# A fused attention and expert kernel: the last pair of heads in two halves of its queries, and other places for three other pieces of work

## The chip, the cores and the metric

The kernel runs on one core of one Trainium2 chip. A core has five engines, each with its own queue of instructions: TensorE (PE in the profile, with its weight loads PEld), VectorE (DVE), ScalarE (ACT), GpSimd (POOL) and SyncE (SP, which here only issues DMAs). An engine takes its instructions in the order in which they are written; a semaphore holds one back until what it needs is done. The metric is the device time of one execution in microseconds (us); lower is better.

## The reference, cut to what matters

```python
# x (4, 1024, 256); 16 heads of 16; 8 experts, top 2, capacity 640
q, k, v = (heads of x @ w.T for w in (wq, wk, wv))
q_mag, k_mag = softplus(q), softplus(k)
q_embed = q_mag * (cos, sin)(pos * inv_freq)               # 32 numbers per head
k_embed = k_mag * (cos, sin)(pos * inv_freq + clip(bias))
attn = softmax(q_embed @ k_embed.T / 4)                    # per batch and head, 1024 x 1024
x = layernorm(x + (attn @ v) @ wo.T)
gates = softmax(x @ router_w + router_b)                   # 4096 tokens, 8 experts
# each token goes to its two best experts; an expert takes its first 640 tokens in order
out = gelu(buf @ w1 + b1) @ w2 + b2                        # per expert, on its 640 slots
x = layernorm(x + sum over the token's experts of gate * out)
```

## The kernel before

**Attention in pairs and steps.** Two heads make a pair. A batch has 8 pairs, the four batches 32 (numbers 0 to 31). A pair is walked in 8 steps of key tiles, 256 steps in all. A *unit* is what is walked at a time: a whole pair (8 steps, all 1024 queries), or half of a pair's queries (4 steps, 512 queries each). Before, the pairs 0 to 3 are walked as two units each, all others as one. `starts` holds the first step of each unit.

In step n of unit w and key tiles c the program writes, in this order: up to two *score* products of a later unit (`score_half`, L755, each followed on DVE by a reduction to a row maximum, L759); `key_scores(w, c, 0)`, two products into a double bank of the pool `st` (L795); a third score; `key_scores(w, c, 1)`; a fourth score; in `exponentials` four short products that subtract the row maxima (L809), and two exponentials of 128x1024 on ACT (L816); `weighted_values` of the step before (av, 16 instructions, L836); further scores; pieces of a later unit's maxima (`max_parts` on DVE and ACT; `max_rows`, four transposes `mp` on PE and a copy `mt` on ACT); and what the table `todo` has for step n. The pool `st` has two buffers, so `key_scores` waits for the exponentials of the step before. Scores use three banks, which they share with the other products.

The scores are spread over the steps by a small plan: each unit's scores must be given two steps before it starts, and each step takes as many as the tightest due time asks for. A whole unit has 32, half a unit 16. Half units need their own maxima, and so their own `max_parts` and `max_rows`.

**Loads.** `load_qk(i)` issues 12 DMAs on SP (8 of 128 KB, 4 of 256 KB), the first six for the pair's first head, the others for the second. Its tile has three buffers, shared with the tables and weights of the lead-in, and with the expert weights. It is called for pair i at the first step of pair i - 2.

**Behind a half batch.** `collect` sends the weighted values and their sums away over SP. `over_sums` then loads the sums (`den`), takes reciprocals on DVE, stores them (`over`), loads them spread over the partitions (`r`, eight DMAs), and multiplies. For the second half of a batch's heads this runs in steps 1, 2, 5 and 6 of the next batch. Then `project` (PE, and an addition on DVE) and `statistics` follow, and `finish_batch`: normalization, transposes, the router, the choice of two experts, the running count of slots, and the indirect DMAs on POOL that scatter the tokens' rows into `slots_in`.

**The end of attention.** The second half of the last batch's heads goes another way: `normalize` (transposes of the av tile, reciprocals and products on DVE into `os`), `turn_back` (transposes of `os`, a copy on ACT), then `project`, `statistics`, and `finish_batch` in two halves of 512 tokens, `one` and `two`. A `run(one)` takes the generator to its next `yield`: reciprocal roots (1), their correction (2), normalizing and transposing (3 to 6), router products (7), and so on to the four scatters of two DMAs each (17 to 20). Only after the last scatter are the first expert's slots loaded (L1183) and transposed (L1194), and the products of the experts begin.

**Lead-in.** Before step 0 the program builds the first pair's queries and keys on the chip. `moving` moves rows into place on PE, with a copy on ACT; `mq1` is the generator for the second half of the queries, `q1` and others are the embeddings. `once` copies weights on DVE and so frees the buffer that pair 1 is loaded into.

Of the kernel before, what the change touches and what calls it, by code (L numbers as in the profile page):

```python
# [10 lines left out]
F32 = mybir.dt.float32  # L11
# [17 lines left out]
def kernel(  # L29
# [72 lines left out]
    with ExitStack() as actx:  # L102
# [627 lines left out]
        nms, mts, avs, pts = {}, {}, {}, {}  # L730


        units = []
        starts, lasting = [], []
        for i in range(B * NU):
            for h in range(2) if i < NU // NF else (None,):
                starts.append(starts[-1] + lasting[-1] if units else 0)
                units.append((i, *divmod(i // (NU // NF), NF), i % (NU // NF), h))
                lasting.append(NT if h is None else NT // 2)
# [158 lines left out]

        def normalize(w, rotate=False):

            _, b, f, p, _ = units[w]
            if p == 0:
                oss[b, f] = p1.tile([P, NT, P], F32, tag="os", name=f"os_{b}_{f}")
            av_sb = avs.pop(w)
            ps = bank(f"avp_{w}", rotate)
            for i in range(4):
                nc.tensor.transpose(
                    ps[:, i * P : (i + 1) * P], av_sb[:, i * P : (i + 1) * P], ident
                )
            r = small.tile([P, 4, 4], F32, tag="rden", name=f"rden_{w}")  # L910
            nc.vector.reciprocal(r, ps.rearrange("p (i s c) -> p i s c", i=4, c=32)[:, :, :, HD])
            for n in range(2):
                nc.vector.tensor_tensor(
                    oss[b, f][:, 4 * n : 4 * (n + 1), 32 * p : 32 * (p + 1)].rearrange(
                        "p i (h d) -> p i h d", d=HD
                    ),
                    ps.rearrange("p (i n h c) -> p n i h c", i=4, n=2, h=2)[:, n, :, :, 0:HD],
                    r[:, :, 2 * n : 2 * n + 2].unsqueeze(3).to_broadcast([P, 4, 2, HD]),
                    ALU.mult,
                )  # L920

# [81 lines left out]
        with tc.manual_schedule():  # L1003
            bias_angles()
            once("k", 0)
            for i in range(2):
                transpose_x(0, i, rotate=True)
            nc.scalar.dma_start(wv_sb, wv)
            for w in "kq":
                load_twice(w, 1, nc.scalar)  # L1010
            for _ in key_table(0):
                pass
            once("q", 0)

            made = {}

            def first(w, h):
                return embedding(
                    0, 0, w, h, fast=(w, h) != ("q", 1), tab=cs if w == "q" else kt0,
                    pauses=(KC - 1,), rotate=True, apart=h == 1, made=made,  # L1020
                )

            def moving(w, h):
                return move_first(w, halves[h], made[w, h])

            k0, q0, k1, q1 = first("k", 0), first("q", 0), first("k", 1), first("q", 1)
            for work in (k0, k0):
                run(work)
            for i in range(2, 4):
                transpose_x(0, i, rotate=True)  # L1030
            table = key_table(1)
            for work in (q0, table, table, q0, k0, table, k1, q0, table, k1):
                run(work)
            mk0, mq0 = moving("k", 0), moving("q", 0)
            for work in (mk0, mq0, mk0, mq0, q1):
                run(work)

            for i in range(2):
                score_half(0, 2 * i, 0, True)
            for work in (k1, q1, q1):  # L1040
                run(work)
            for i in range(2, 4):
                score_half(0, 2 * i, 0, True)
            for work in (mk0, mq0, mk0, mq0, k0, q0):
                run(work)
            mk1 = moving("k", 1)
            run(mk1)
            for i in range(4):
                score_half(0, 2 * i + 1, 0, True)
            for work in (mk1, mk1, mk1, k1):  # L1050
                run(work)
            vals = [values_in_two(0, 0, h, rotate=True) for h in range(2)]
            for h in range(2):
                for i in range(4):
                    score_half(0, 2 * i + h, 1, True)
                    if (h, i) in ((0, 3), (1, 1)):
                        run(vals[0])
            for _ in vals[1]:
                pass
            mq1 = moving("q", 1)  # L1060
            for _ in range(4):
                run(mq1)
            for _ in max_parts(0):
                pass
            max_rows(0, rotate=True)
            run(q1)
            for h in range(2):
                store_table(0, h, cs[:, :, halves[h]])
                store_table(1, h, kt0[:, :, halves[h]])
            once("k", 1)  # L1070
            once("q", 1)
            load_qk(1)
            late_constants()
# [10 lines left out]
        with tc.manual_schedule():  # L1084
            for n in range(NS):
                w, c = step_of[n]
                b, p, t = n // (NU * NT), n // NT % NU, n % NT
                if n % NT == 0 and n > 0 or n == NT // 2:
                    i = n // NT + 2
                    if i < B * NU:  # L1090
                        load_qk(i)
                    elif i - B * NU < 2:
                        experts[i - B * NU] = expert_weights(i - B * NU)


                third_last, others[0] = others[0], False
                items = [(score_half, *x) for x in ahead[n]]
                first, third, fourth, rest = items[:2], items[2:3], items[3:4], items[4:]
                if third_last:
                    third, fourth = [], third + fourth  # L1100
                for f, *args in first:
                    f(*args)
                if parts:
                    run(parts)
                    parts = None
                tiles = [key_scores(w, c, 0)]
                for f, *args in third:
                    f(*args)
                tiles.append(key_scores(w, c, 1))
                for f, *args in fourth:  # L1110
                    f(*args)
                exponentials(w, c, tiles)
                if n > 0:
                    weighted_values(*step_of[n - 1])
                for f, *args in rest:
                    f(*args)
                if n + 2 in starts:
                    parts = max_parts(starts.index(n + 2))
                    run(parts)
                if n + 1 in starts:  # L1120
                    max_rows(starts.index(n + 1))
                if c == 1 and w > 0 and not by_rows(w - 1):
                    normalize(w - 1)
                for f, args in todo.get(n, ()):
                    f(*args)
                if b > 0 and (p, t) in FINISH:
                    if b not in finishing:
                        finishing[b] = finish_batch(b - 1)
                    next(finishing[b], None)
            weighted_values(*step_of[NS - 1])  # L1130


        with tc.manual_schedule():
            b, n = B - 1, NT // 2
            normalize(len(units) - 1, rotate=True)
            for i in range(2):
                turn_back(b, 1, i, rotate=True)
            for j in range(2):
                project(b, 1, j, rotate=True)
                statistics(b, j)  # L1140
            one, two = (finish_batch(b, rotate=True, lo=lo, n=n) for lo in (0, n))
            run(one)
            project(b, 1, 2, rotate=True)
            for _ in range(3):
                run(one)
            project(b, 1, 3, rotate=True)
            for j in range(2, 4):
                statistics(b, j)
            for _ in range(3):
                run(one)  # L1150
            run(two)
            for _ in range(2):
                run(one)
            run(two)
            for _ in range(4):
                run(one)
            run(two)
            for _ in range(3):
                run(one)
            for _ in range(n):  # L1160
                run(one)
            for _ in two:
                pass
            second_factors()
            nc.scalar.preload_act_table_set("gelu_and_others")
# [297 lines left out]
```

## Time and profile before

| What | Value |
|---|---|
| median of 3 runs | 1423.62 us (1423.34 to 1423.67) |
| the profiled execution | 1425.13 us |
| its span, first to last instruction | 1423.3 us |
| PE busy | 1365.4 us (96%) |
| DVE busy | 885.8 us (62%) |
| ACT busy | 740.8 us (52%) |
| POOL busy | 408.3 us (29%) |
| score products (L755), 1024 | 383.4 us busy, mean 434 ns |
| score reductions (L759), 1024 | 646.9 us busy, mean 683 ns |
| mean granted TensorE clock | 0.983 |

All durations come from one profiled execution. Busy times of PE are modelled at their ends, so a busy PE is not PE at its peak; step lengths are therefore read as distances between the starts of the same instruction in two steps. In section 2 of the page the span is cut into 40 slices of 35.6 us, and a digit is the busy share of a slice in tenths; PEclk is the clock that TensorE was granted. A timeline line has the start, the duration, engine, line, operation, what it writes and reads, and in square brackets how long the engine was idle before it and what ended that. SPq lines are DMA issues. A table by stage has from:to, length, then for PE, PEld, DVE, ACT and POOL the busy time and number of instructions, then clock, share of the DMA engines and GB/s.

### The profile page before, as it was taken

What the parts mean: (1) busy time and instruction counts of PE and PEld (TensorE: products, weight loads), DVE (VectorE), ACT (ScalarE), POOL (GpSimd) and SP (SyncE); (2) the same over time, 40 slices, a digit from 0 to 9 for tenths busy, and PEclk for the clock granted to TensorE, in tenths of its full rate; (3) what the DMA queues carried; (4) which work ended last, traced back from release to release, by engine and by line L of the source; (5) the groups of instructions that cost most, each with busy time, mean ns of one, the idle gap of its engine ahead of it and who ended that gap; (6) DMA issues with size and microseconds to landing.
All of it is one profiled execution on the core that took longest, in us unless ns stands there. A gap on an engine that the chain in (4) does not pass through costs nothing. (4 is left out here: it accounts for less than half of the span.)

```text
span 1423.3 us, 24542 instructions
## 1 busy us (share of the span) xinstructions
PE 1365.4 (96%) x9362; PEld 863.9 (61%) x9362; DVE 885.8 (62%) x1931; ACT 740.8 (52%) x1025; POOL 408.3 (29%) x427
## 2 busy tenths in 40 slices
PE   7999999999999999999999999999996399999998
PEld 4655555655655565565556556655643277777776
DVE  7667666667876666777856577887734433333335
ACT  5665676565566656556575665656463122222221
POOL 5261043340002646100065530000310314444443
PEclk9999999999999999999999999999998599999999
DMA  6776476374543746454466462225210436334211
GB/s 192 214 206 194 141 200 189 86 228 113 138 123 96 229 143 182 112 165 97 139 184 193 106 186 70 64 74 128 75 66 1 141 114 207 111 117 135 84 44 56
DMA packets 107765, 190.20 MB, mean 134 GB/s; under 512 B 19553, under 2 KB 56642, under 8 KB 107520
## 3 DMA queue, kind: packets, MB, share of 16 engines
q1 hardware_dynamic: 97792, 169.90, 41.2%
q0 software_dynamic: 8736, 16.87, 3.9%
q10 hardware_dynamic: 1120, 1.87, 0.4%
q8 instruction: 74, 1.21, 0.4%
q14 instruction: 43, 0.35, 0.1%
HBM read 118.27 MB, written 73.63 MB: 135 GB/s over the span
## 5 line engine op out<-in xcount | busy, mean ns | idle before, releaser
L759 DVE TENSOR_REDUCE nm<-s 128x1 f32<-128x512 f32 x1024 | 646.9, 683 | 234.1 <-PE s L755 226.0
L816 ACT ACTIVATE pt<-st 128x1024 f32<-128x1024 f32 x512 | 496.1, 1021 | 364.1 <-PE st L809 363.6
L755 PE MATMUL s<-qk 128*128 128x512 f32 x1024 | 383.4, 434 | 3.6 <-DVE nm L759 2.2
L795 PE MATMUL st<-qk 128*128 128x512 f32 x1024 | 303.8, 398 | 2.6 <-ACT pt L816 2.6
L836 PE MATMUL av<-pt,va 128*32 128x256 f32 x4096 | 274.7, 385 | 0.5 <-ACT pt L816 0.5
L755 PEld LDWEIGHTS s<-qk 128*128 128x128 f32 x1024 | 177.9, 188 | 110.5 <-DVE nm L759 49.4
L795 PEld LDWEIGHTS st<-qk 128*128 128x128 f32 x1024 | 182.7, 188 | 63.5 <-ACT pt L816 29.2
L836 PEld LDWEIGHTS av<-pt,va 128*32 128x32 f32 x4096 | 107.1, 109 | 107.0 <-issue 61.6
L692 POOL DMA_INDIRECT slots_in<-held,scatter_idx x64 | 63.0, 984 | 290.9 <-DVE scatter_idx L688 213.6
L414 POOL TENSOR_TENSOR soft_q<-y_q,soft_q 128x512 f32<-128x512 f32 x15 | 19.3, 1285 | 439.7 <-ACT soft_q L410 439.7
L1364 PE MATMUL op<-w,h 128*128 128x256 f32 x640 | 144.1, 379 | 0.0
L1345 PE MATMUL hp<-slots_t,w 128*128 128x320 f32 x512 | 141.0, 437 | 0.0
L1364 PEld LDWEIGHTS op<-w,h 128*128 128x128 f32 x640 | 119.5, 190 | 15.9
L809 PE MATMUL st<-mt,ones_r 2*128 2x512 f32 x1024 | 128.8, 492 | 0.0
L1345 PEld LDWEIGHTS hp<-slots_t,w 128*128 128x128 f32 x512 | 98.4, 192 | 40.4 <-issue 1.0
L809 PEld LDWEIGHTS st<-mt,ones_r 2*128 2x128 f32 x1024 | 49.0, 182 | 88.5 <-issue 88.1
L1352 ACT ACTIVATE h<-hp,b_sb 128x640 f32<-128x640 f32 x64 | 50.8, 793 | 87.7 <-PE hp L1345 87.7
L1379 DVE TENSOR_TENSOR o<-op,b_sb 128x256 f32<-128x256 f32 x35 | 14.9, 424 | 94.7 <-PE op L1364 94.6
L1380 ACT ACTIVATE o<-o,w 128x256 f32<-128x256 f32 x35 | 17.8, 508 | 103.2 <-issue 72.3
L1382 POOL DMA_INDIRECT y_rank<-o,rows x35 | 35.9, 1024 | 101.2 <-ACT slots_t L1195 46.1
L1303 POOL DMA_INDIRECT out_dram<-row,rows x40 | 40.9, 1022 | 42.7 <-DMA out_dram<-row,rows 13.1
L420 POOL TENSOR_TENSOR e_k<-soft_k,tab_k 128x512 f32<-128x512 f32 x28 | 35.4, 1286 | 47.5 <-DMA tab_k<-table 47.1
(217 smaller groups left out, 1034.5 us busy)
## 6 DMA issues: line engine op xcount, KB each, us to landing
qk<-embed_q SPq DMA_DIRECT2D x248, 128.0 KB
qk<-embed_k SPq DMA_DIRECT2D x124, 256.0 KB
embed_k<-parts_k SPq DMA_DIRECT2D x64, 256.0 KB
embed_q<-parts_q SPq DMA_DIRECT2D x64, 256.0 KB
w<-in_w_dram SPq DMA_DIRECT2D x16, 1024.0 KB
y_rank<-zero SPq DMA_DIRECT2D x8, 1024.0 KB
tab_q<-table SPq DMA_DIRECT2D x14, 512.0 KB
tab_k<-table SPq DMA_DIRECT2D x14, 512.0 KB
```

Of the source, the lines that this page charges most:

```text
L692: nc.gpsimd.indirect_dma_start(out=scatter_views[2 * t + k], out_offset=bass.IndirectOffsetOnAxis(ap=scatter_idx[:, k, t : t + 1], axis=0) ...
L755: nc.tensor.matmul(ps, qk[:, 2 * h, lo : lo + P], qk[:, 2 * h + 1, j * HS : (j + 1) * HS], start=True, stop=True,)
L759: nc.vector.tensor_reduce(nms[w][:, i, s, j : j + 1], ps, AX.X, ALU.max, negate=True)
L795: nc.tensor.matmul(ps[:, x, :], qk[:, 2 * h + 1, k * P : (k + 1) * P], qk[:, 2 * h, q * HS : (q + 1) * HS], start=True, stop=False,)
L809: nc.tensor.matmul(tiles[t][:, x, :], ones_r[rows, :], mts[w][rows, :], start=False, stop=True,)
L816: nc.scalar.activation(pt, tiles[t], AF.Exp)
L836: nc.tensor.matmul(av[32 * s : 32 * (s + 1), to], va[f][:, k, 2 * p + h, :], e, start=(c == 0 and n == 0), stop=(last and n == 1),)
L1303: nc.gpsimd.indirect_dma_start(out=out_views[t], out_offset=bass.IndirectOffsetOnAxis(ap=to[:, 0, t : t + 1], axis=0), in_=row[:, t, :], i ...
L1345: nc.tensor.matmul(ps[:, i, 0:half], w1_sb[:, k, c * P : (c + 1) * P], s_t[:, k, i * half : (i + 1) * half], start=(k == 0), stop=(k == KC ...
L1352: nc.scalar.activation(h_t[:, c, :].rearrange("p (i n) -> p i n", i=2), ps[:, :, 0:half], AF.Gelu, bias=b1_sb[:, e, c : c + 1],)
L1364: nc.tensor.matmul(ps, h_t[:, c, t * P : (t + 1) * P], w2_sb[:, c, :], start=(c == 0), stop=(c == HC - 1),)
L1382: nc.gpsimd.indirect_dma_start(out=y_views[e * ST + t], out_offset=bass.IndirectOffsetOnAxis(ap=to[:, 1, t : t + 1], axis=0), in_=o_sb, in ...
```

## The change

Pair 31 is walked as two half units, and pairs 1 to 3 as whole units; pair 0 stays in halves. `normalize` can take half a unit. In step 253 the first half of pair 31 is normalized, at the start of step 254 its tokens are turned back, at that step's end tiles 0 to 3 are projected and their statistics taken, and in step 255 `one` makes its first stage. The order of what follows attention is rewritten accordingly. In the lead-in, `max_parts(0)` comes before the second half of the values, and three of the four stages of `mq1` come after `max_rows(0)`. The qk load at the first step of a batch (other than batch 0) moves to the batch's fourth step.

```diff
--- before.py
+++ after.py
@@ -730,10 +730,12 @@
         nms, mts, avs, pts = {}, {}, {}, {}
 
 
+
+        BY_HALF = (0, B * NU - 1)
         units = []
         starts, lasting = [], []
         for i in range(B * NU):
-            for h in range(2) if i < NU // NF else (None,):
+            for h in range(2) if i in BY_HALF else (None,):
                 starts.append(starts[-1] + lasting[-1] if units else 0)
                 units.append((i, *divmod(i // (NU // NF), NF), i % (NU // NF), h))
                 lasting.append(NT if h is None else NT // 2)
@@ -898,24 +900,27 @@
 
         def normalize(w, rotate=False):
 
-            _, b, f, p, _ = units[w]
+            _, b, f, p, half = units[w]
             if p == 0:
                 oss[b, f] = p1.tile([P, NT, P], F32, tag="os", name=f"os_{b}_{f}")
             av_sb = avs.pop(w)
             ps = bank(f"avp_{w}", rotate)
-            for i in range(4):
+
+            m, tiles = (4, (0, 4)) if half is None else (2, (4 * half, 4 * half + 2))
+            for i in range(m):
                 nc.tensor.transpose(
                     ps[:, i * P : (i + 1) * P], av_sb[:, i * P : (i + 1) * P], ident
                 )
-            r = small.tile([P, 4, 4], F32, tag="rden", name=f"rden_{w}")
-            nc.vector.reciprocal(r, ps.rearrange("p (i s c) -> p i s c", i=4, c=32)[:, :, :, HD])
-            for n in range(2):
+            ps = ps[:, 0 : m * P]
+            r = small.tile([P, 4, 4], F32, tag="rden", name=f"rden_{w}")[:, 0:m, :]
+            nc.vector.reciprocal(r, ps.rearrange("p (i s c) -> p i s c", i=m, c=32)[:, :, :, HD])
+            for n, t in enumerate(tiles):
                 nc.vector.tensor_tensor(
-                    oss[b, f][:, 4 * n : 4 * (n + 1), 32 * p : 32 * (p + 1)].rearrange(
+                    oss[b, f][:, t : t + m, 32 * p : 32 * (p + 1)].rearrange(
                         "p i (h d) -> p i h d", d=HD
                     ),
-                    ps.rearrange("p (i n h c) -> p n i h c", i=4, n=2, h=2)[:, n, :, :, 0:HD],
-                    r[:, :, 2 * n : 2 * n + 2].unsqueeze(3).to_broadcast([P, 4, 2, HD]),
+                    ps.rearrange("p (i n h c) -> p n i h c", i=m, n=2, h=2)[:, n, :, :, 0:HD],
+                    r[:, :, 2 * n : 2 * n + 2].unsqueeze(3).to_broadcast([P, m, 2, HD]),
                     ALU.mult,
                 )
 
@@ -1055,15 +1060,15 @@
                     score_half(0, 2 * i + h, 1, True)
                     if (h, i) in ((0, 3), (1, 1)):
                         run(vals[0])
+            for _ in max_parts(0):
+                pass
             for _ in vals[1]:
                 pass
             mq1 = moving("q", 1)
-            for _ in range(4):
-                run(mq1)
-            for _ in max_parts(0):
-                pass
+            run(mq1)
             max_rows(0, rotate=True)
-            run(q1)
+            for work in (mq1, mq1, mq1, q1):
+                run(work)
             for h in range(2):
                 store_table(0, h, cs[:, :, halves[h]])
                 store_table(1, h, kt0[:, :, halves[h]])
@@ -1085,12 +1090,15 @@
             for n in range(NS):
                 w, c = step_of[n]
                 b, p, t = n // (NU * NT), n // NT % NU, n % NT
-                if n % NT == 0 and n > 0 or n == NT // 2:
+
+                if t == 0 and p > 0 or t == 3 and p == 0 and b > 0 or n == NT // 2:
                     i = n // NT + 2
                     if i < B * NU:
                         load_qk(i)
                     elif i - B * NU < 2:
                         experts[i - B * NU] = expert_weights(i - B * NU)
+                if n == NS - 2:
+                    turn_back(B - 1, 1, 0)
 
 
                 third_last, others[0] = others[0], False
@@ -1127,27 +1135,31 @@
                     if b not in finishing:
                         finishing[b] = finish_batch(b - 1)
                     next(finishing[b], None)
+                if n == NS - 2:
+                    for j in range(2):
+                        project(b, 1, j)
+                        statistics(b, j)
+                    one, two = (
+                        finish_batch(b, rotate=True, lo=lo, n=NT // 2) for lo in (0, NT // 2)
+                    )
+                elif n == NS - 1:
+                    run(one)
             weighted_values(*step_of[NS - 1])
 
 
         with tc.manual_schedule():
             b, n = B - 1, NT // 2
+            run(one)
             normalize(len(units) - 1, rotate=True)
-            for i in range(2):
-                turn_back(b, 1, i, rotate=True)
-            for j in range(2):
+            for _ in range(2):
+                run(one)
+            turn_back(b, 1, 1, rotate=True)
+            for _ in range(2):
+                run(one)
+            for j in range(2, 4):
                 project(b, 1, j, rotate=True)
                 statistics(b, j)
-            one, two = (finish_batch(b, rotate=True, lo=lo, n=n) for lo in (0, n))
             run(one)
-            project(b, 1, 2, rotate=True)
-            for _ in range(3):
-                run(one)
-            project(b, 1, 3, rotate=True)
-            for j in range(2, 4):
-                statistics(b, j)
-            for _ in range(3):
-                run(one)
             run(two)
             for _ in range(2):
                 run(one)
```

## The prediction

> **What bounds the kernel now.** I read the page first, then TensorE's timeline by steps, the timeline of the passage between attention and experts, and SyncE's timeline where a batch begins.
>
> ```profile
> span 1423.3 us, 24542 instructions
> ...
> PE   7999999999999999999999999999996399999998
> ...
> PEclk9999999999999999999999999999998599999999
> ```
>
> PE is busy in every slice but those around 1067 to 1139 us, and there the granted clock drops too. Elsewhere a change pays only if it takes work or a wait from PE. Steps, from the timeline:
>
> ```profile
> 1034.94 1.07 PE L836 MATMUL av<-pt,va 128*32 128x256 f32 x16
> ...
> 1038.44 1.07 PE L836 MATMUL av<-pt,va 128*32 128x256 f32 x16
> ...
> 1063.92 0.73 PE L795 MATMUL st<-qk 128*128 128x512 f32 x2 [0.19 <-ACT pt L816]
> ...
> 1065.02 1.07 PE L836 MATMUL av<-pt,va 128*32 128x256 f32 x16
> 1068.28 1.07 PE L836 MATMUL av<-pt,va 128*32 128x256 f32 x16
> ```
>
> Four score products: 3.50 us from one av group to the next, no gap on PE. No scores (the last nine steps): still 3.26, because the second st pair waits for the second exponential. Five scores take 3.85 (69.08 to 72.92 in the same view). So a score costs 0.35 where PE is full and nothing below a floor of about 3.2.
>
> The passage, all engines:
>
> ```profile
> 1071.72 1.94 ACT L816 ACTIVATE pt<-st 128x1024 f32<-128x1024 f32 x2 [1.33 <-PE st L809]
> ...
> 1092.36 0.19 DVE L604 TENSOR_TENSOR logits<-lq,rb_sb 128x32 f32<-128x32 f32 x1 [0.18 <-PE lq L590]
> ...
> 1100.52 0.97 POOL L692 DMA_INDIRECT slots_in<-held,scatter_idx  x1 [62.46 <-DVE held L678]
> ...
> 1112.32 0.97 POOL L692 DMA_INDIRECT slots_in<-held,scatter_idx  x1 [1.89 <-DVE second L706]
> ...
> 1123.93 0.94 SPq L1183 DMA_DIRECT2D slots<-slots_in  x2
> ...
> 1128.18 3.00 PE L1194 MATMUL st<-ident,slots 128*128 128x128 f32 x10 [17.92 <-DMA slots<-slots_in]
> ```
>
> One serial chain: step 254's exponentials, routing of the first half, eight scatters, routing of the second half (late by 1.89), eight scatters, reload. The start of batch 1, SyncE and DVE:
>
> ```profile
> 311.52 2.98 SPq L485 DMA_DIRECT2D qk<-embed_q  x4
> ...
> 321.88 0.49 SPq L872 DMA_DIRECT2D sums<-avs  x1
> 324.66 0.34 SPq L882 DMA_DIRECT2D den<-sums  x1
> 327.04 0.34 SPq L886 DMA_DIRECT2D over<-den  x1
> 328.51 4.33 SPq L889 DMA_DIRECT2D r<-over  x8
> 341.84 1.71 SPq L485 DMA_DIRECT2D qk<-embed_q  x4
> ```
> ```profile
> 326.46 0.55 DVE L884 RECIPROCAL den<-den 128x64 f32<-128x64 f32 x1 [1.93 <-DMA den<-sums]
> ```
>
> The qk load stands ahead of the sums; the reciprocal comes late, score reductions queue behind it on DVE, and PE's step takes 4.47 instead of 3.50 (av at 324.01, then 328.48). In batch 2 it loses 1.18 likewise, in batch 3 nothing. Of a load itself the table by stage says:
>
> ```profile
> 350.00:352.00 2.00, 2.00 (x18) 1.14 (x20) 2.00 (x5) 0.16 (x1) 0.00 (x0) 1.00 0.98 240
> 352.00:354.00 2.00, 2.00 (x22) 1.36 (x15) 0.70 (x2) 1.78 (x2) 0.00 (x0) 1.00 0.25 53
> ```
>
> The load issued from 341.84 moves data until about 352.5: 10.7 us from first issue to last byte.
>
> **Passage, first half early: -5.6, and +0.7.** Count from step 254's exponentials (before: 1071.72; logits 20.6 later). After: two projections (0.78 each, 999.86 to 1000.64) go between its av and the next st, so step 255's exponentials start at 4.0 instead of 3.25 and end at 5.95. The sums and statistics of tiles 0 to 3 (1.81 per projection on DVE, 1082.68 to 1084.49) run from 1.7 to 5.3, hidden beside them. Then half a unit is left: 8 of 16 av products (0.55), copy 0.38, two transposes and the division to 8.1, turn-back and copy 1.35 to 9.4, beside it the four normalizing rows on DVE (1.38, from 1087.86); x1's transposes stand before the projections, to 10.0; DVE gets the third projection 1.1 later (1081.51 to 1082.68), two times 1.81 gives 14.7, logits 15.0: 5.6 earlier. From there the order is unchanged, 8.2 to the first scatter, 11.8 more to the ninth. The scatters on POOL (1.28 apart) follow at the same distances, so all 5.6 reach the reload. Cost: in step 253 the turn-back stands before the st pair and waits for the division (0.75 on DVE); that pair and the exponentials queue behind it and come 4.0 after this step's instead of 3.26, +0.7. ACT's extra copies fit in its 1.3 idle per step. Bounds: 4 to 7 for the gain.
>
> **Clock.** It is half from about 1090 and returns inside 1130 to 1140 (0.76 there), some 6.6 after the 1128.18 product; I keep that, at 0. [...]
>
> **Last pair by half: -2.2.** Its 32 scores go 3 to a step for eight steps and 2 for four instead of 4 for eight. Eight steps fall from 3.50 to 3.17 (PE alone) or 3.26 (the floor): 1.9 to 2.6. The 2-score steps lie under the floor, and the second row of maxima with them.
>
> **Pairs 1 to 3 whole: -0.3.** The diff's new condition also makes these whole. Steps 0 to 6 get 7 scores (6 in the last) where they had 5 (6 in the first), steps 7 to 18 get 4 where they had 5. Twelve more at 0.27 (three in 0.80 at 69.08) is +3.2, twelve fewer at 0.35 is -4.2; three rows of maxima fewer at 0.39 (3.89 against 3.50) is -1.2. Seven put three scores at a step's end and two at the next's start on three banks; DVE takes 0.62 for each, so the fourth and fifth wait, about 0.8 together, in some 3.5 steps: +2.8. Two stalls (0.55 at 89.84, 0.32 at 163.21) go: -0.9. Not seen in the trace at 7; I bound it by -2 and +3.
>
> **Lead-in: -0.7.** PE idles 1.12 before mp at 42.20. In the new order mp stands between the two row moves with its input long ready, but ACT copies mt before the query rows, so the first score starts near 41.9, not 42.61. Bounds 0 and -1.1. The weights' copies on DVE, which release pair 1's buffer, come earlier too; pair 1 is needed a step sooner and still in time.
>
> **Loads at a batch's start: +2.3.** The early load goes; sums are stored from 317.9 (avs copied 317.84), the reciprocal no longer waits, and PE gains 0.97 and 1.18: -2.15. But the load now stands behind den, over and eight r loads. Sums end 321.4, den 1.2 later (as in batch 3), reciprocal 324.5, over 325.1, r 326.6 to 330.9, load from 330.95; with 10.7 to 10.8 it lands at 341.7. Its pair is first scored in step 71 (339.92 before, 339.0 after), its second head at 340.0. PE waits 1.7; the same count gives 1.75 and 1.05 in batches 2 and 3: +4.5; behind the waiting score stand that step's second st pair and both exponentials. Behind the load on SyncE stands only pair 11's, issued from 341.84. If den comes 2.3 after the sums and the load takes 11.7 (573.68, data until 585.4) it is 11; if it lands within 9.1, nothing. [...]
>
> **Sum.** -5.6 + 0.7 - 2.2 - 0.3 - 0.7 + 2.3 = -5.8. The profiled execution took 1425.13 with a span of 1423.3, the median is 1423.62; the difference applies to both: 1417.8, its own range 1414 to 1421.5.
>
> **Rivals.** Loads land in time (0.2): the queue is emptier at the fourth step, no wait: -10.3, 1413.3. Against it, the loads measured in the trace so take 10.7 to 11.8. Passage gains only half (0.16): if what follows the logits, not DVE's statistics, sets the scatters; the 1.89 gap on POOL speaks for the chain, the half clock could stretch it: -3, 1420.6. Slower (0.08): the late load is the new bound. A load among other stores took 14.3 (76.69 to 91.0); at that, PE waits 5.1 per batch, 15.3 in all, and the sum is +5: 1428.6. It decides from 4.5 us per batch on; against it, no stores are queued there.
>
> **Numbers.** The forecast has 0.56. A measurement tells 0.2%, 2.8 us, from no change: faster means below 1420.8. Forecast 0.47 of its 0.56, the timely loads 0.2, the half passage 0.05: 0.72. Slower 0.08, the rest 0.20. The range 1412 to 1423 leaves out the slow rival and some of the tails.
>
> **What would show it.** Right: PE waits of 1 to 2 us at scores behind the qk load about seven steps after each batch's start; den waits gone; steps 239 to 246 at 3.2; first scatter about 23.2 after step 254's exponentials (28.8 before); av groups near 5 us apart in the first steps. Wrong: no such PE waits (then near 1413), or over 4 each, or the ninth scatter not moved.

## The result, and the profile after

No change that can be measured. The changed kernel took 1425.64 us in the median of 22 runs (1422.16 to 1430.54), the kernel before, run beside it, 1426.08; the ratio is 1.0002 (95% interval 0.9993 to 1.0010). In a second set of runs it was 1.0005 (0.9993 to 1.0017). The forecast was 1417.8, range 1412 to 1423. The profiled execution took 1427.6, 2.0 above the median, with a span of 1425.8; 2.5 more than that of before.

The page answers with almost the same lines. PEclk reads a 9 ahead of its 5 where it read an 8; nothing in 40 slices shows what happened in the middle of attention:

```profile
span 1425.8 us, 24478 instructions
...
PE   7999999999999999999999999999996399999998
...
PEclk9999999999999999999999999999999599999999
```

So I compared step by step: the start of the products that subtract the row maxima (L809 before, L811 after), one start for each of the 256 steps. D is the start after, less the start before, in the profiled executions:

| Stretch | D at its start and end | Change | Predicted |
|---|---|---|---|
| lead-in, step 0 | 0 to -0.69 | -0.69 | -0.7 |
| steps 0 to 64 (pairs 1 to 3 whole) | -0.69 to -0.54, with +6.86 at step 7 | +0.15 | -0.3 |
| steps 64 to 237 (three batch starts) | -0.54 to 10.80 | +11.3 | +2.3 |
| steps 237 to 253 (last pair) | 10.80 to 8.95 | -1.9 | -2.2 |
| step 253 to 254 (turn-back) | 8.95 to 9.62 | +0.7 | +0.7 |
| from there to the first slots' transposes | 9.62 to 3.97 | -5.65 | -5.6 |
| from there to the end | 3.97 to 2.5 | -1.5 | 0 |

Five rows came within half a microsecond, the last within 1.5. One did not: at +11.3 it outweighs the 8.9 that the others gained together. Its size varies: in a second profiled execution of the same kernel (below) it is +7.5 (-0.80 to 6.69).

**The rows that held.** TensorE's timeline of the last pair, and the passage from the timeline of all engines; these answer to the lines at 1034.94 and 1071.72 of before.

```profile
1044.35 1.07 PE L838 MATMUL av<-pt,va 128*32 128x256 f32 x16
1047.60 1.07 PE L838 MATMUL av<-pt,va 128*32 128x256 f32 x16
```
```profile
1081.33 1.94 ACT L818 ACTIVATE pt<-st 128x1024 f32<-128x1024 f32 x2 [0.77 <-PE st L811]
...
1096.30 0.18 DVE L604 TENSOR_TENSOR logits<-lq,rb_sb 128x32 f32<-128x32 f32 x1
1104.51 0.97 POOL L692 DMA_INDIRECT slots_in<-held,scatter_idx  x1 [56.86 <-DVE held L678]
...
1116.32 0.97 POOL L692 DMA_INDIRECT slots_in<-held,scatter_idx  x1 [1.89 <-DVE second L706]
...
1132.15 3.01 PE L1206 MATMUL st<-ident,slots 128*128 128x128 f32 x10 [17.89 <-DMA slots<-slots_in]
```

A step with three scores is 3.25 long where one with four was 3.50: the floor, as assumed. From step 254's exponentials to the logits it is now 14.97 (20.64 before), to the first scatter 23.2 (28.8), and the gaps of 1.89 and 17.9 behind them are those of before.

**The row that failed.** SyncE's and DVE's timelines at the start of batch 1, which answer to those at 311.52 and 326.46:

```profile
321.93 0.32 SPq L884 DMA_DIRECT2D den<-sums  x1
324.48 0.33 SPq L888 DMA_DIRECT2D over<-den  x1
325.96 3.60 SPq L891 DMA_DIRECT2D r<-over  x8
329.66 1.76 SPq L485 DMA_DIRECT2D qk<-embed_q  x4
```
```profile
323.91 0.54 DVE L886 RECIPROCAL den<-den 128x64 f32<-128x64 f32 x1
```

The reciprocal waits for nothing now, and D falls by 0.96 at step 67, as predicted. The load goes out at 329.66, 1.3 earlier than predicted. Yet TensorE's timeline, and the table by stage (clock third from the end), read:

```profile
341.72 0.47 PE L757 MATMUL s<-qk 128*128 128x512 f32 x1 [2.03 <-DMA qk<-embed_k]
...
343.25 1.59 PE L838 MATMUL av<-pt,va 128*32 128x256 f32 x16
```
```profile
342.00:344.00 2.00, 2.00 (x20) 1.07 (x22) 1.38 (x2) 0.57 (x1) 0.00 (x0) 0.92 0.12 33
344.00:346.00 2.00, 2.00 (x13) 1.23 (x6) 0.00 (x0) 1.45 (x3) 0.00 (x0) 0.50 0.83 240
346.00:348.00 2.00, 2.00 (x8) 1.57 (x8) 0.56 (x1) 0.51 (x1) 0.00 (x0) 0.73 0.97 248
```

Two things are to be seen. The product of the second head waits 2.03 us for the load. And after the wait the same 16 av products take 1.59 instead of 1.07: the granted clock is at one half from 343.66 to 347.07, for 3.41 us in which TensorE has no gap at all. The three batch starts cost 3.80, 5.69 and 3.74. The waits are 2.03, 2.56 and 2.14 of that; the half clock lasts 3.41, 6.83 and 3.41. If half of such a stretch is lost, that is 1.7, 3.4 and 1.7, which with the waits gives 3.7, 6.0 and 3.8.

### The profile page after: what moved, and what is told of

Its sections match the earlier page's. It is cut to its first block, busy times and chain, and to the rows that moved or that the text cites. A ratio compares the mean times of both kernels' runs of the same rounds, so it can differ in the third digit from the quotient of the medians.

```text
span 1425.8 us, 24478 instructions
## 1 busy us (share of the span) xinstructions
PE 1365.1 (96%) x9354; PEld 864.8 (61%) x9354; DVE 886.6 (62%) x1930; ACT 739.1 (52%) x1017; POOL 408.4 (29%) x427
## 5 line engine op out<-in xcount | busy, mean ns | idle before, releaser
L811 PE MATMUL st<-mt,ones_r 2*128 2x512 f32 x1024 | 129.4, 495 | 0.0
L811 PEld LDWEIGHTS st<-mt,ones_r 2*128 2x128 f32 x1024 | 49.3, 183 | 89.6 <-issue 88.9
L514 DVE TENSOR_TENSOR held<-po,held 128x512 f32<-128x512 f32 x32 | 22.1, 690 | 50.0 <-PE po L506 50.0
```

The source lines that it names most:

```text
L811: nc.tensor.matmul(tiles[t][:, x, :], ones_r[rows, :], mts[w][rows, :], start=False, stop=True,)
```

## The experiments

Theory: the late load alone undoes the change, by its waits and by the clock that each wait costs; the rest is worth about what was predicted for it. The rival: the loads are not the cause, and the passage's gain is lost elsewhere or in the spread of runs. Twelve experiments were run in three sets of four. Ratios are to the kernel before, run in the same set, whose medians were 1436.05, 1426.04 and 1427.42; microseconds beside a ratio are its distance from 1, times that median. The expectations speak of chips instead of sets; the record numbers the chips 9, 15 and 9, and does not tell whether both 9s are one chip.

### The change without its late load, twice

```diff
-  if t == 0 and p > 0 or t == 3 and p == 0 and b > 0 or n == NT // 2:
+  if n % NT == 0 and n > 0 or n == NT // 2:
```

> The changed kernel with the loads as before: at every first step of a pair, a batch's first included. Theory (the late load costs waits, and each wait then costs clock): no wait of a score for the qk load, no stretch in the middle of attention with the clock near 0.5 after steps 71, 135 and 199; the reciprocal's stall of about 0.7 us a batch is back. The other parts of the change stay: lead-in -0.7, last pair -2.1, passage -5.6, turn-back and projections +1.9, front +0.2, clock's return up to -1.5. In the profile the time is 6.3 to 8 us below the kernel before; by medians the same. Rival (the loads are not the cause, the passage's gain is lost to a run-to-run spread or to something else in the last pair): within 2 us of the kernel before, and of the changed kernel.

Measured: 0.9938 (0.9921 to 0.9955), -8.9 us. No wait for a load, no half clock at the batch starts. In the first set all four kernels were held back in other places too (see the end), so it was run again in the third:

> The changed kernel with the loads as before, on this chip. On the first chip it was measured on, late signals of TensorE at steps 110 and 174 disturbed all kernels. Theory: 6.5 to 9 us faster than the kernel before; the kernel with the later sums was 10.2 faster, and 2.2 us of that are the reciprocal's stall, so -8 is the middle. Rival (the first chip's -9.4 was its disturbance): under 4 us.

Measured: 0.9943 (0.9925 to 0.9961), -8.1 us; its profiled execution took 1415.89. The rival falls: give the load its old place, and the change gains what was forecast and a little more.

### The late load alone, twice

```diff
-  if n % NT == 0 and n > 0 or n == NT // 2:
+  if t == 0 and p > 0 or t == 3 and p == 0 and b > 0 or n == NT // 2:
```

> The kernel before with nothing but the late load at a batch's start (fourth step in place of the first). Theory: three waits of a score for the qk load, 2 to 2.6 us each, none of the reciprocal, and after each wait a stretch of 3 to 7 us in which the granted clock is near 0.5; slower than the kernel before by 4.5 us (waits alone, less the stalls of the reciprocal) to 11 us (with the clock), by runs that fall on either side in phase. Rival (loads not the cause): within 2 us of the kernel before.

Measured: 1.0061 (1.0042 to 1.0079), +8.8 us, with waits of 2.35, 2.78 and 2.69 and the half clock behind all three.

> The kernel before with nothing but the late load, on this chip. Theory (the parts add): what the loads back gain and what the late load costs sum to about what the whole change does, 0: 6 to 9 us slower than the kernel before. Rival (the late load costs only in company of the other parts, or only on the first chip): under 3 us.

Measured: 1.0063 (1.0041 to 1.0086), +9.0 us, waits of 2.42, 2.28 and 2.42, half clock for 6.83 us behind each. The two parts add: -8.9 and +8.8 in the first set, -8.1 and +9.0 in the third. That is the nothing that the whole change measured.

### The changed kernel again, and the wait filled

> The changed kernel itself, unchanged, on the chip on which the next ones run. Theory: the same as the kernel before within 2 us, with three waits of a score for the late load (2 to 3 us each) and the half clock behind them. If the two parts add (the first runs gave -9.4 for the change without its late load and +8.9 for the late load alone), it is -0.5. Rival: on another chip the load lands otherwise, and the time moves from that of the kernel before by more than 3 us.

Measured: 1.0005 (0.9993 to 1.0017). Its trace brought a natural control. It waits three times, 2.50, 2.28 and 1.99 us, and only the first is followed by the half clock (342.41 to 345.82). The second, from TensorE's timeline and the table by stage:

```profile
606.43 0.47 PE L757 MATMUL s<-qk 128*128 128x512 f32 x1 [2.28 <-issue]
```
```profile
606.00:608.00 2.00, 1.57 (x12) 0.90 (x14) 1.06 (x2) 0.00 (x0) 0.00 (x0) 1.00 0.00 0
608.00:610.00 2.00, 2.00 (x27) 1.36 (x24) 0.32 (x1) 1.86 (x3) 0.00 (x0) 1.00 0.76 219
```

(`issue` means that the profile names nothing that ended the wait; the product and the place are the same.) Here D rises by 2.5, the wait and little else; at the first, with a wait only 0.2 longer, it rises by 4.2. The same edit costs about 1.7 more or not. This fits the spread of the changed kernel's runs, 7.6 us between the ends of the twelve in this set.

Then the wait was kept and TensorE given work in it:

```diff
                 tiles = [key_scores(w, c, 0)]
+                if b > 0 and p == 0 and t == 7:
+                    ps = bank(f"fill_{n}")
+                    for _ in range(8):
+                        nc.tensor.matmul(
+                            ps, ones_r, qks[units[w][0]][:, 0, 0:HS], start=True, stop=True
+                        )
                 for f, *args in third:
```

> The changed kernel, with eight products of 128x512 that nothing reads, from the pair's current qk tile into a score bank, ahead of the third score of the step in which the late load is waited for (about 2 us of work at full clock, three times). They lie in the time of the wait, so that TensorE does not stand idle. Theory, its part on the clock (idle time of TensorE brings the half clock): the waits all but go, the fill takes about their place, no stretch near 0.5 in the middle of attention; against the changed kernel faster by 4 to 6.5 us in the profile, although it does more work. Rival (the half clock there has another cause than the idle time, or costs nothing): the stretches stay, and the time is that of the changed kernel or up to 2 us more.

Measured: 0.9978 (0.9963 to 0.9994), -3.2 us. In the second set, beside the changed kernel itself:

> The filled wait once more, beside the changed kernel itself on the same chip: eight unread products three times in the time of the wait for the late load. Theory (idle time of TensorE brings the half clock): faster than the changed kernel by 2 to 5 us although the waits' time is still spent, none of the half clock in the middle of attention. Rival (no effect of idle time on the clock that costs anything): the same time as the changed kernel or up to 2 us more.

Measured: 0.9973 (0.9963 to 0.9984), -3.9 us, where the changed kernel had +0.7; the intervals do not meet. These nine runs spread over 2.3 us. TensorE's timeline of this kernel at the place of the failed row:

```profile
338.57 2.03 PE L1118 MATMUL fill<-qk,ones_r 128*128 128x512 f32 x8
341.13 0.47 PE L757 MATMUL s<-qk 128*128 128x512 f32 x1 [0.53 <-DMA qk<-embed_k]
...
342.65 1.07 PE L838 MATMUL av<-pt,va 128*32 128x256 f32 x16
```

The load is as late as ever, but the av products behind it take 1.07. In both runs of this kernel none of the six places has a half clock. Useless work made the kernel faster.

The control puts the same products behind the waiting one (after `tiles.append(key_scores(w, c, 1))`):

> The control to the filled wait: the same eight unread products three times, but written behind the product that waits for the late load instead of ahead of it. The same work is added, the wait is not filled. Theory (idle time brings the half clock): waits of 2 to 3 us and half-clock stretches as in the changed kernel, plus the products' time of 2 us each or more at half clock: 5 to 8 us slower than the kernel before, 9 to 12 slower than with the fill ahead. Rival (the products themselves help, wherever they stand): the same time as with the fill ahead, 3 to 5 us faster than the kernel before.

Measured: 1.0029 (1.0018 to 1.0040), +4.1 us, below the 5 to 8 expected, but on the theory's side:

```profile
340.69 0.47 PE L757 MATMUL s<-qk 128*128 128x512 f32 x1 [1.90 <-DMA qk<-embed_k]
...
341.46 3.21 PE L1121 MATMUL fill<-qk,ones_r 128*128 128x512 f32 x8
```

The eight products take 3.21 where they took 2.03 ahead of the wait, and the half clock follows all three waits. At the three batch starts D rises by 18.3 with the fill behind and by 7.8 with it ahead, a difference of 10.5; three times 2.03 us, the products at full clock, would account for 6 of it. So it is not the products that help, but that they stand where TensorE would have been idle.

### The load one step earlier, and the sums one step later

> The changed kernel with the late load one step earlier (third step in place of the fourth), and the third and fourth piece of the sums behind a half batch one step later (steps 6 and 7 in place of 5 and 6 for the last, 2 unchanged). Theory: the load starts about 3.5 us earlier and so lands about 1.5 us before the second head's first score needs it: no wait of a score for it, no half clock, and the reciprocal's stall of 0.7 us a batch stays away; 8 to 9 us faster than the kernel before in the profile. Rival (the load, wherever it is put between the sums' DMAs, delays them or is delayed): a stall of 0.7 us or more a batch in the reciprocal or the projection, and a time no better than with the loads as before.

(Its sums behind a half batch come in steps 1, 2, 6 and 7 instead of 1, 2, 5 and 6.) Measured: 0.9957 (0.9942 to 0.9973), -6.2 us, short of the 8 to 9 expected. No wait for the load, but the rival was partly right: the load now stands ahead of `over` and `r` in SyncE's queue, the multiplication by `r` waits on DVE (1.70 us in batch 3), and steps 70, 134 and 198 take 0.5, 0.4 and 1.2 longer. The stall that the late load was to remove moved.

The other way to remove it is to leave the load alone and take the reciprocal later (on top of the loads back):

```diff
-            for c in (1, 2, 5, 6):
+            for c in (1, 3, 6, 7):
                 at(b, 0, c, run, pieces)
```

> The changed kernel with the loads as before (first step of each pair), and the reciprocal of the sums behind a half batch moved instead: its four pieces in steps 1, 3, 6 and 7 of the next batch in place of 1, 2, 5 and 6. That takes the same stall away that the late load took away (0.97, 1.2 and near 0 us), without a load that comes late. Theory: no wait for a load and none of the reciprocal; 8.7 to 11 us faster than the kernel before, the fastest of all. Rival (the sums that now come a step later hold back the projection, as the third-step load did by 0.4 to 1.2 us a batch): 7 to 9 us, no better than the loads back alone.

Measured: 1415.81 us, ratio 0.9925 (0.9911 to 0.9938), -10.7 us: the fastest of all, with runs from 1414.43 to 1416.55 only. Its interval overlaps those of the loads back; what it has over them is shown by the trace, where D falls by about 1.0 and 1.2 at steps 67 and 131 with nothing paid for it. The reciprocal on DVE, first in the kernel with the loads back (third set), then here:

```profile
325.28 0.55 DVE L886 RECIPROCAL den<-den 128x64 f32<-128x64 f32 x1 [2.20 <-DMA den<-sums]
```
```profile
327.56 0.54 DVE L886 RECIPROCAL den<-den 128x64 f32<-128x64 f32 x1
```

It comes when `den` is there, and holds nobody back. This kernel beats both the kernel before and the changed one.

### The end alone, the front alone

> The kernel before with only the end of attention changed: pair 31 by half, its first half normalized, turned back, projected beside the second half, and the new order behind it. Pairs 1 to 3 stay in halves, lead-in and loads as before. Theory, from the trace of the changed kernel: pair 31 -2.1, turn-back and projections +2.0 of which the passage's gap contains 1, passage -5.6, earlier return of the clock -1.5, in all -8.3 in the profile from step 239 to the end, nothing before it. Rival (the end's gain was lost, and the changed kernel's other parts gained what the loads cost): within 3 us of the kernel before.

Measured: 0.9953 (0.9938 to 0.9968), -6.7 us. Short of the 8.3 expected, and the trace says where: four small waits of TensorE at the very end of attention (0.18, 0.28, 0.49 and 0.65) here were followed by a half clock of 3.41 us from 1080.01 on, and the logits came 1.4 later than in the changed kernel, counted from step 254; the load of the first slots took another 0.6. Together this is the 2.0 by which the passage gained 3.7 instead of 5.65. In the nine other profiled executions with the new end it gained 5.6 to 5.7.

> The kernel before with only the two early parts of the change: pairs 1 to 3 as whole units, and the lead-in in its new order. Loads and the end of attention as before. Theory, from the traces of the kernels that have these parts: step 0 starts 0.3 to 1.2 us earlier or not at all, the stalls of steps 1 to 7 (up to 7 us) are given back by step 32, and nothing is left: -0.7 to +0.3 us. Rival (whole pairs gain or cost something that the other parts hid): a difference of 2 us or more.

Measured: 0.9990 (0.9978 to 1.0002), -1.4 us: below the -0.7 to +0.3 expected, but not told from no change. Its D is -0.82 at step 0, +6.58 at step 7 and -0.99 at step 30. End and front sum to -8.1, what the change without the late load measured.

## Why the prediction was wrong

**The step that failed: "Loads at a batch's start: +2.3".** Its direction was right and its first half exact: the reciprocal's stall went (-0.96 and -1.2 for -0.97 and -1.18). Its second half, "+4.5" for three waits of 1.7, 1.75 and 1.05, was mis-sized in two ways.

- The waits were 2.03, 2.56 and 2.14, 6.7 in all. In batch 1 the load went out 1.3 earlier than counted, and its data moved for about 10.8 us, as counted; but I let TensorE go on with the last byte. The table by stage shows the DMA engines all but idle from 340.5 on, and the product starts at 341.72, some 1.2 us later:

```profile
340.50:341.00 0.50, 0.00 (x0) 0.00 (x0) 0.00 (x0) 0.00 (x0) 0.00 (x0) 1.00 0.04 8
341.00:341.50 0.50, 0.00 (x0) 0.00 (x0) 0.00 (x0) 0.00 (x0) 0.00 (x0) 1.00 0.00 0
```

These two errors cancel in batch 1 (341.72, where 341.7 was counted); its wait is longer because TensorE came 0.3 earlier. In all three, 12.0 to 12.5 us pass from the first issue to the waiting product, where 10.7 to 10.8 were counted. Waits make 2.2 of the miss.

- I priced a wait at its length, and the clock behind it at nothing. TensorE's clock fell after each, which cost 6.5 more. This mechanism stood in the prediction for the passage only. It is the larger part of the miss in this execution: with 2.2 + 6.5 the term is +11.0. In the second profiled execution the waits are as long (6.8), but only one is followed by the half clock, and what goes beyond the waits is 2.4. By the ratios, the kernel with the wait filled was 4.6 us faster than the changed kernel in the same set.

**The slower rival** had the place right ("the late load is the new bound") and by chance came near the price: it wanted 5.1 per batch and 15.3 in all, and the two profiled executions have 13.2 and 9.1. But its mechanism, a load of 14.3 us, was not seen. The rival of a load in time (0.2) is excluded: this product waited 1.9 to 2.9 us in every one of the 15 places without a fill ahead of it; in eleven the profile names the load as what ended the wait, in four it names nothing.

**Passage, turn-back, last pair, lead-in** held to within 0.4 us each, and the experiments with the loads back show them in the time, not only in the trace: 8.1 to 8.9. The passage's rival ("gains only half") is excluded; the chain through DVE's statistics fits, with 5.6 to 5.7 in nine of the ten traces. The lead-in's -0.7 fits, though a single start says little: step 0 began 0.25 to 2.04 earlier in ten profiled kernels with the new order (mean 1.06), and between 0.42 earlier and 0.24 later in three with the old one.

**Clock.** I kept the return 6.6 us after the experts' first product. It came 3.4 after it in the changed kernel (1135.55) and 6.2 in its second run, so it gave 1.5 once and almost nothing the other time. In all fourteen traces it came 3.4 to 6.7 after that product, a spread of 3.3. That is just under the 3.41 us of the grid on which these traces show the clock change (last section), so the return looks like a matter of phase, and no single figure for it holds.

**Pairs 1 to 3.** The stalls of the first steps were under-counted (D rises by 7.6 up to step 7), and so was what comes back. The balance of +0.15 is near the forecast -0.3, but its parts were not: that agreement is in part luck.

## What to carry to other kernels

In these traces a wait of TensorE has two prices: its length, and, when 1.79 us of idleness or more fell into one window of 3.41 us (between 1.42 and 1.69: two times in six; the windows are those of the next section), a clock at one half for 3.41 or 6.83 us, of which half is lost by my estimate. Where TensorE was otherwise full, waits of 2.0 to 2.8 us therefore cost 2.5 to 5.9, and the phase decided, which fits the spread of runs: 7.6 us for the changed kernel, 2.3 with the wait filled in the same set. Before a load is moved later, count to the instruction that uses it with about a microsecond behind the last byte (here 1.2); and ask whether the stall that is to go can be removed by moving its own victim, which here cost nothing.

## What the runs showed of the hardware

**The clock's windows.** In all traces the changes of the granted clock within one execution lie on a grid of 3.41 us (in the changed kernel at 343.66, 347.07, 606.49, 613.31, 872.73, 876.14). I divided attention, from 60 us to 6 us after the last step's start, into these windows in all fourteen traces and summed TensorE's idle time in each. Of the windows at full clock, all 17 with 1.79 us or more of it were followed by half clock; none with 1.29 or less was; of six between 1.42 and 1.69, two. (TensorE's ends are modelled, which may blur the border.) One of these two is the changed kernel's window from 340.25 to 343.66: 1.47 us of idleness in 3.41, so less than half a window was enough there. The second wait of the repeated changed kernel, 2.28 us, fell across a border, 1.08 and 1.20, and cost nothing more. Why a stretch lasts one window (3.41 us) or two (6.83 us) was not settled.

**Late signals in one set of runs.** In all four kernels of the first set, what waits for TensorE's products went on late in step 110 (the copy on ACT 2.8 to 3.2 us behind their recorded end; 0.03 in the kernel before), again in step 174, and less so from step 238 on, 64 steps or one batch apart. In the kernel with the loads back, products of 498.97 to 501.02 let ACT go on only at 503.93:

```profile
498.97 2.05 PE L360 MATMUL vp<-wv_sb,xt 128*128 128x128 f32 x16
...
503.93 0.58 ACT L369 COPY va<-vp 128x512 f32<-128x512 f32 x1 [3.64 <-remote]
```

DVE was held at the same moment. In that profile the three places cost 5.5 (with a half clock of 6.83 us), 2.6 and 2.5 us; the kernel before had its slowest median, 1436.05, in this set. In the other two sets these places are undisturbed, in the third too, whose chip has the same number in the record. The cause is open, and so is whether it lies in the chip.
